# A metaformer kernel with gathers on GpSimd: readers of PSUM wait for a slot's last product

## The chip, the cores and the metric

The kernel runs on one core of one Trainium2 chip. The metric is the device time of one execution in microseconds (us); lower is better. The engines are called by their names in the profile where rows are quoted: PE is TensorE, DVE is VectorE, ACT is ScalarE, POOL is GpSimd, SP is SyncE; PEld is TensorE's loading of weights.

## What is computed

The reference is a network of two layers on four images of 128 channels and 128 x 128 pixels, in 32-bit floats. Layer 0 normalises, computes 18 offsets per pixel by a 3 x 3 convolution, reads each of nine taps at an offset position by bilinear interpolation, and multiplies the taps with a weight matrix (a deformable convolution). Its second half sends each token to the two best of eight experts. Layer 1 has a spectral convolution, which the kernel computes as products with a fixed matrix on flipped and plain channels, and a soft mixture of the eight best of 64 experts.

```python
def corner(iy, ix, w):
    valid = (iy >= 0) & (iy <= H - 1) & (ix >= 0) & (ix <= W - 1)
    iyc = jnp.clip(iy, 0, H - 1).astype(jnp.int32)
    ixc = jnp.clip(ix, 0, W - 1).astype(jnp.int32)
    g = jax.vmap(lambda img, yy, xx: img[:, yy, xx])(x, iyc, ixc)
    return g * (w * valid.astype(x.dtype))[:, None]
return corner(y0, x0, wy0 * wx0) + corner(y0, x1, wy0 * wx1) + corner(y1, x0, wy1 * wx0) + corner(y1, x1, wy1 * wx1)
...
return jnp.einsum('bckhw,ock->bohw', sampled, w_conv.reshape(O, C, K * K))
```

## The kernel before

**Slots.** An image is cut into 32 groups of four rows, and a row's nine taps into three chunks of three taps. One chunk is one slot: 12 slots to a group, 384 to an image, 1536 in the main loop (`while n < total + 3 or turns.jobs`, from L1588). The class `Chunk` (L729 to L786) holds what is done for one chunk, in the order of its life:

- `gather` (L737): three indirect DMAs, one per tap, issued by GpSimd. Each fetches for the 128 pixels of a row the four corners of 128 channels, out of a table in HBM, into the tile `g`. There are seven such tiles (`AHEAD`).
- `weighted` (L750): VectorE multiplies the corners by their weights, two taps or three. The weights are in the tile `spread`.
- `weighted_too` (L758): for chunks past the first of a row, ScalarE weights the third tap, with four activations.
- `summed` (L766): twelve transposes on TensorE, four per tap, add up the corners in a bank of PSUM, the tile `trg`.
- `moved` (L780): ScalarE copies `trg` to `sT` in SBUF; after the fourth row of a group a job is started that multiplies `sT` with the weights of the convolution, into the PSUM tile `sums`.

In slot n the loop does, in this order: `weighted` of chunk n+1, `moved` of chunk n-2, a step of each job that is due, the weights of a group, `weighted_too` of chunk n+1, `summed` of chunk n, the fillings of banks by jobs, and last the gather of chunk n+7, when the chunk is appended to the list.

**Jobs.** All other work (the experts, the normalisations, the offsets of the next image) is written as generators, which the class `Turns` (L114 to L156) resumes. A job yields `FILL` before it fills a bank and a number of slots before it reads one. In the main loop `turns.hop` is 2: a bank is read two slots after it was filled. Before and after the loop it is 1. A PSUM pool has six banks (`BANKS`); `fills` lets jobs fill no more than these in two slots. [...]

**Order.** `InOrder` (L91 to L103) wraps each engine and keeps its instructions in the order of the program, so every operation has the line L101 in the profile, and rows are told apart by their tiles. Semaphores are placed by the framework from reads and writes of tiles: a reader of a bank waits for the products that filled it, the next filling waits for the readers and the earlier products, and a gather waits for the transposes that read its tile `g` last.

```python
def issued(*args, **kwargs):
    return self.tc.keep_in_program_order(issue(*args, **kwargs))
```

Of the kernel before, what the change touches and what calls it, by code (L numbers as in the profile page):

```python
# [42 lines left out]
F32 = mybir.dt.float32  # L43
# [5 lines left out]
PSUM = bass.MemoryType.PSUM  # L49
# [41 lines left out]
class InOrder:  # L91


    def __init__(self, tc, engine):
        self.tc, self.engine = tc, engine

    def __getattr__(self, name):
        issue = getattr(self.engine, name)

        def issued(*args, **kwargs):  # L100
            return self.tc.keep_in_program_order(issue(*args, **kwargs))  # L101

        return issued  # L103


class Engines:
    def __init__(self, tc):
        nc = tc.nc
        self.tensor, self.vector = InOrder(tc, nc.tensor), InOrder(tc, nc.vector)
        self.scalar, self.gpsimd = InOrder(tc, nc.scalar), InOrder(tc, nc.gpsimd)  # L110
        self.sync = InOrder(tc, nc.sync)


# [73 lines left out]
def metaformer_kernel(  # L187
# [16 lines left out]
    nc = tc.nc  # L204
# [33 lines left out]
    with ExitStack() as main:  # L238
# [7 lines left out]
        p_x = main.enter_context(tc.tile_pool(name="p_x", bufs=BANKS, space=PSUM))  # L246
# [2 lines left out]

        def bank(shape, name):  # L250

            return p_x.tile(shape, F32, name=name, tag="bank")

        eng = Engines(tc)
        turns = Turns()
# [4 lines left out]
        class Image:  # L260


            def __init__(self, b):
                self.b = b
                self.table = tabs.tile([TW * TC, 2 * P], F32, name=f"table{b}", tag="table")
                self.grid = self.table.rearrange("(i j) e -> i j e", j=TC)
                self.index = pw.tile([P, P, TAPS], I32, name=f"index{b}", tag="index")
                self.weight = {}
                self.xc = {}
                self.z = {}  # L270
                self.tails = {}


                self.read = self.normed = self.continued = self.sent = 0
                self.offsets = self.placed = self.known = 0
                self.left = 0
                self.direct = P // RB
                self.rooms = {}

            def room(self, q):  # L280
                return pw.tile(
                    [P, CB, TAPS, 4],
                    F32,
                    name=f"weight{self.b}_{q}",
                    tag="weight",
                    bufs=3 * P // CB // 2,
                )
# [372 lines left out]
        def table_of(im, pitch):  # L660

            base = turns.slot
            im.left = P // RB + 1 + P // CB
            for t in range(P // RB + 1):
                while turns.slot < base + int(t * pitch):
                    yield 1
                turns.start(block(im, t))

        def later_offsets(im):
            for t in range(im.direct, P // RB):  # L670
                turns.start(again(im, t))
                yield SPACE
# [56 lines left out]
        class Chunk:  # L729
# [7 lines left out]
            def gather(self):  # L737
                self.g = pg.tile([P, 3, 4, P], F32, name="g", tag="g")
                for i in range(3):
                    k = self.k0 + i  # L740
                    eng.gpsimd.indirect_dma_start(
                        out=self.g[:, i].rearrange("p s c -> p (s c)"),
                        out_offset=None,
                        in_=self.row.group.im.table,
                        in_offset=bass.IndirectOffsetOnAxis(
                            ap=self.row.group.im.index[:, self.row.y, k : k + 1], axis=0
                        ),
                    )

            def weighted(self):  # L750
                n = 2 if self.shared else 3
                gf = self.g[:, 0:n].rearrange("p k s c -> p (k s) c")
                w = self.row.group.w[:, self.row.s, 4 * self.k0 : 4 * (self.k0 + n)]
                eng.vector.tensor_tensor(
                    gf, gf, w.unsqueeze(2).to_broadcast(list(gf.shape)), ALU.mult
                )
# [830 lines left out]
        n = -1  # L1587
        while n < total + 3 or turns.jobs:  # L1588
            turns.slot = start + n
            b, k = divmod(n, slots)  # L1590
            if n == 0:
                turns.start(later_offsets(first))
            lag = 0 if b else SPACE * (P // RB - AFTER + 2)
            if k == lag and b + 1 < NB:
                images[b + 1] = Image(b + 1)
                images[b + 1].border()
                pitch = (slots - AHEAD - BLOCK - lag) / (P // RB)
                turns.start(table_of(images[b + 1], pitch))
            if n + 1 < total:
                chunk[n + 1].weighted()  # L1600
            if 0 <= n - 2 < total:
                chunk[n - 2].moved()
            turns.steps()
            if n >= 0 and n + 3 < total and (n + 3) % 12 == 0:
                chunk[n + 3].row.group.weights((n + 3) // 12 % 2)
            if n + 1 < total and chunk[n + 1].shared:
                chunk[n + 1].weighted_too()
            if 0 <= n < total:
                chunk[n].summed()
                turns.fill()  # L1610
            turns.fills(0)
            if n == LATE * slots:

                phase_a.close()
                late = main.enter_context(tc.tile_pool(name="late", bufs=2, side="right"))
                b1T = late.tile([P, NJ, E1], F32, name="b1T", tag="b1T", bufs=1)
                b2T = late.tile([P, E1], F32, name="b2T", tag="b2T", bufs=1)
                turns.start(biases(), later=True)
                part = lambda: late.tile([P, 2, HID], F32, name="w", tag="w", bufs=4)

                rooms = [[part(), part()], [part(), part()], flat_pads]
                rooms.append([pw.tile([P, 2, HID], F32, name="w", tag="index")])
                for _ in range(2):
                    rooms[-1].append(
                        pw.tile([P, 1, HID], F32, name="w", tag="weight", bufs=3 * P // CB // 2)
                    )
                middle = Experts(range(LATE), Weights(lambda i: rooms[i % 4]), 4, 2)
                middle.part = part
                middle.streams = 2
                middle.weights.load(4)  # L1630
                middle.start()
            if 0 <= n - 2 < total:
                chunk[n - 2] = None
            if 0 <= n and len(chunk) < total:
                chunk.append(next(source))
            n += 1
            if n == total + 2:
                turns.hop = 1

                sampling.close()  # L1640
                own = main.enter_context(tc.tile_pool(name="own", bufs=OWN))

                flat = lambda w: w[:, 0:8, :].rearrange("p (n q) c -> p n (q c)", q=4)
                others = [
                    flat_pads,
                    [(late, f"{tile}{b}") for tile in ("tok", "share") for b in (1, 2)],
                    [flat(wconv_sb), flat(ew_sb)],
                ]

                def room(i):  # L1650
                    i %= OWN + 3 + len(LEFT)
                    if i < OWN:
                        return own.tile([P, EC, HID], F32, name="w", tag="w")
                    i -= OWN
                    if i == 1:
                        return [
                            pool.tile([P, 1, HID], F32, name="w", tag=tag, bufs=1)
                            for pool, tag in others[1]
                        ]
                    if i < 3:  # L1660
                        return others[i]
                    return [
                        pb.tile([P, n, HID], F32, name="w", tag=tag, bufs=bufs)
                        for tag, n, bufs in LEFT[i - 3]
                    ]

                ending = Ending(range(LATE, NB), Weights(room), OWN + 2, 1)
                ending.part = lambda: own.tile([P, 2, HID], F32, name="w", tag="w")
                ending.streams = OWN // 2
                ending.among = False  # L1670
                turns.start(ahead())
                ending.start()
# [39 lines left out]
```

## Time and profile before

| what | value |
|---|---|
| median of three runs | 7361.9 us (7357.83 to 7363.09) |
| the profiled execution, its own time | 7358.05 us |
| span in its profile, first to last instruction | 7356.1 us |
| mean granted clock of TensorE | 0.896 |
| busy: TensorE, VectorE, ScalarE, GpSimd | 82%, 65%, 50%, 60% |
| gathers by GpSimd | 4608, of 950 ns |
| copies of `trg` to `sT` by ScalarE | 1536, of 472 ns |
| transposes into `trg` | 18432 |

A group row of the profile has the line, the engine, the operation, the tiles written and read with their shapes, and the count; after the first bar the busy time and the mean duration in ns; after the second the time that the engine sat idle just before these instructions, and what ended most of it. "issue" there is time in which an engine waited for nothing that the profile shows, and "remote" a signal whose sender it doesn't name. A row of the timeline has the start, the duration, the engine, the operation and its tiles, and in brackets the idle time before it. In the 40 slices of the span the shares hardly change from the second slice to the last but one: TensorE is 80 to 90% busy in most, GpSimd 60%. 1536 slots fill nearly the whole span.

### The profile page before, as it was taken

The page shows a single profiled execution, that of the slowest core. Times are in us where ns is not written, and L with a number is a line of the kernel's source. Part 1 is how long each engine was busy: PE and PEld are TensorE (multiplying, and loading weights), DVE is VectorE, ACT ScalarE, POOL GpSimd, SP SyncE. Part 2 cuts the span into 40 slices and gives each one's busy share as a digit, 9 for nine tenths or more (in the row PEclk, how much of TensorE's full clock was granted, in tenths as well). Part 3 has the DMA queues.
Part 4 walks back from the last instruction along what each step waited for, and adds up shares of the span by engine and source line. Part 5 has one row for each costly group of instructions (what it writes and reads, how often), then busy time and mean ns, then how long its engine had stood idle before and what let it go on. Part 6 is the DMA issues. An engine that isn't in the chain of part 4 may idle for free. (4 is left out here: it accounts for less than half of the span.)

```text
span 7356.1 us, 103037 instructions
## 1 busy us (share of the span) xinstructions
PE 6006.3 (82%) x31271; PEld 3981.9 (54%) x31271; DVE 4789.5 (65%) x16100; ACT 3707.7 (50%) x9999; POOL 4432.3 (60%) x4691
## 2 busy tenths in 40 slices
PE   5788888887888888887888888888877788788885
PEld 3455555555555555555555555555555555555553
DVE  5466666676667666666667666667667665566663
ACT  4345555554555555554455555555444444444452
POOL 1666666666666666666666666666666665666641
PEclk7888999998898998998899999898898999899897
DMA  6666666666666666666666666666666677677777
GB/s 204 191 200 212 204 207 210 202 194 188 197 201 203 205 206 200 204 193 186 193 209 200 207 202 201 198 199 210 186 189 181 201 250 238 180 247 237 246 236 273
DMA packets 578917, 1524.69 MB, mean 207 GB/s; under 512 B 86424, under 2 KB 225408, under 8 KB 578368
## 3 DMA queue, kind: packets, MB, share of 16 engines
q0 software_dynamic: 369664, 1210.35, 55.0%
q1 hardware_dynamic: 206400, 299.36, 12.1%
q10 hardware_dynamic: 2304, 8.39, 0.3%
q8 instruction: 254, 4.16, 0.2%
q14 instruction: 295, 2.42, 0.1%
HBM read 1380.92 MB, written 136.85 MB: 206 GB/s over the span
## 5 line engine op out<-in xcount | busy, mean ns | idle before, releaser
L101 POOL DMA_INDIRECT g<-table,index x4608 | 4377.4, 950 | 2710.4 <-issue 1190.9
L101 PEld LDWEIGHTS trg<-ident,g 128*128 128x128 f32 x18432 | 2300.2, 150 | 1501.3 <-issue 1288.2
L101 PE MATMUL trg<-ident,g 128*128 128x128 f32 x18432 | 2575.2, 288 | 562.9 <-issue 465.9
L101 DVE SCALAR_TENSOR_TENSOR x<-pe,scaled,x 128x128 f32<-128x128 f32 x4048 | 1379.7, 341 | 1432.5 <-remote 644.6
L101 DVE TENSOR_TENSOR g<-g,spread 128x1024 f32<-128x1024 f32 (+1 forms) x1536 | 2129.1, 1387 | 202.4 <-DMA g<-table,index 90.0
L101 ACT COPY sT<-trg 128x384 f32<-128x384 f32 x1536 | 720.5, 472 | 2742.1 <-remote 1187.4
L101 PE MATMUL sums<-sT,wconv_sb 128*128 128x512 f32 x2304 | 1326.6, 658 | 53.1 <-issue 50.9
L101 ACT ACTIVATE g<-g,weight 128x128 f32<-128x128 f32 x4096 | 1306.3, 394 | 1.9 <-DMA g<-table,index 1.7
L101 PE MATMUL pe<-ew_sb,x1T 128*128 128x512 f32 x2048 | 1163.6, 649 | 147.0 <-issue 88.6
L101 PEld LDWEIGHTS sums<-sT,wconv_sb 128*128 128x128 f32 x2304 | 435.1, 208 | 518.9 <-issue 516.5
L101 PEld LDWEIGHTS pe<-ew_sb,x1T 128*128 128x128 f32 x2048 | 343.7, 205 | 261.1 <-issue 182.3
L101 ACT ACT_TABLE_LOAD x270 | 346.4, 1283 | 23.5 <-DVE nmax L101 9.8
L101 PE MATMUL sums<-xg,ident 128*128 128x512 f32 x256 | 163.8, 726 | 125.8 <-ACT x1T L101 96.8
L101 DVE TENSOR_TENSOR x<-ps,x 128x512 f32<-128x512 f32 x128 | 88.1, 688 | 264.5 <-remote 119.6
L101 PE MATMUL po<-pad,woff_sb 128*64 128x512 f32 x768 | 216.1, 645 | 17.8 <-issue 11.0
L101 DVE TENSOR_TENSOR x<-x,pe 128x512 f32<-128x512 f32 x128 | 87.0, 679 | 217.8 <-remote 130.4
L101 PE MATMUL pl<-rw_sb,x1T 128*128 128x8 f32 x1024 | 143.9, 256 | 98.2 <-issue 88.7
L101 ACT ACTIVATE tn<-x,d_nb,d_rs 128x128 f32<-128x128 f32 x512 | 211.2, 487 | 5.5 <-DVE x L101 2.6
L101 ACT ACTIVATE xn<-x,c_nb,c_rs 128x128 f32<-128x128 f32 x512 | 210.6, 485 | 4.7 <-issue 1.8
L101 PEld LDWEIGHTS pl<-rw_sb,x1T 128*128 128x128 f32 x1024 | 147.3, 213 | 98.5 <-issue 88.6
L101 ACT ACTIVATE ent<-raw,a_nb,a_rs 128x128 f32<-128x128 f32 x448 | 185.0, 485 | 7.6 <-remote 3.8
L101 PE MATMUL pe<-eb_sb,gT 32*128 32x512 f32 x256 | 169.4, 740 | 20.0 <-issue 14.6
(227 smaller groups left out, 5130.9 us busy)
## 6 DMA issues: line engine op xcount, KB each, us to landing
g<-table,index POOLq DMA_INDIRECT x4608
table<-ent SPq DMA_DIRECT2D x64, 1024.0 KB
xc<-in_x SPq DMA_DIRECT2D x64, 512.0 KB
w<-x_d SPq DMA_DIRECT2D x64, 512.0 KB
xg<-in_x SPq DMA_DIRECT2D x124, 256.0 KB
x_d<-x SPq DMA_DIRECT2D x124, 256.0 KB
out<-w SPq DMA_DIRECT2D x48, 512.0 KB
w<-in_weight SPq DMA_DIRECT2D x40, 512.0 KB
```

The lines of the kernel that those rows point to most:

```text
L101: return self.tc.keep_in_program_order(issue(*args, **kwargs))
```

## The change

The wrappers of the engines get state. `Fills`, on TensorE, keeps the last product issued, the last product of each of the last three slots (`ends`), and the products that went into each tile. `Readers`, on VectorE, ScalarE and GpSimd, looks at each instruction that reads a PSUM tile which TensorE filled:

- The first such reader of a slot on ScalarE, and the first on VectorE, gets a wait for `ends[-2]`, the last product of two slots ago. This holds in the main loop only (`turns.hop` over 1). Later readers in the slot are behind it in their engine's order.
- A reader that reads at least four fifths of a tile, or a tile with one product only, becomes its fence: the products of the tile are put in a group without dependencies among them, and the reader stands for it. The bank's next filling waits for that reader.
- The first of a chunk's three gathers gets a wait for `ends[-1]`, the last product of the slot that has just been issued.

The loop marks the first readers as `fresh` at the start of each slot and calls `eng.tensor.end()` after the fillings. No arithmetic, no transfer and no tile is changed.

```diff
+class Fills(InOrder):
+    def __init__(self, tc, engine):
+        super().__init__(tc, engine)
+        self.last, self.ends = None, []
+        self.sizes, self.of = {}, {}
...
+            made = issue(*args, **kwargs)
+            self.last = made.ins
+            self.of.setdefault(args[0].name, []).append(made.ins)
+            return made
...
+    def end(self):
+        self.ends = self.ends[-2:] + [self.last]
+
+class Readers(InOrder):
...
+    def behind(self, made, end):
+        self.tc.add_manual_dep(
+            made.ins,
+            end.name,
+            mybir.DependencyInfo(mybir.DependencyClass.Sync, mybir.DependencyReason.DATA),
+        )
+
+    def read(self, made, a):
+        if self.fresh:
+            self.behind(made, self.fills.ends[-2])
+            self.fresh = False
+        made_of, size = self.fills.of[a.name], self.fills.sizes.get(a.name)
+        if size and (len(made_of) == 1 or 5 * a.free_size() >= 4 * size):
+            for ins in made_of:
+                self.tc.add_to_no_dep_group(a.name, ins)
+            self.tc.declare_fence(made.ins, group=a.name)
+            del self.fills.sizes[a.name]
...
+            for a in list(args) + list(kwargs.values()):
+                if isinstance(a, bass.AP) and a.space == PSUM and a.name in self.fills.of:
+                    self.read(made, a)
+                    break
...
 class Engines:
     def __init__(self, tc):
         nc = tc.nc
-        self.tensor, self.vector = InOrder(tc, nc.tensor), InOrder(tc, nc.vector)
-        self.scalar, self.gpsimd = InOrder(tc, nc.scalar), InOrder(tc, nc.gpsimd)
+        self.tensor = Fills(tc, nc.tensor)
+        self.vector, self.scalar, self.gpsimd = (
+            Readers(tc, engine, self.tensor) for engine in (nc.vector, nc.scalar, nc.gpsimd)
+        )
...
-            return p_x.tile(shape, F32, name=name, tag="bank")
+            tile = p_x.tile(shape, F32, name=name, tag="bank")
+            eng.tensor.sizes[tile.name] = tile.free_size()
+            return tile
...
-                    eng.gpsimd.indirect_dma_start(
+                    made = eng.gpsimd.indirect_dma_start(
...
+                    if i == 0 and eng.tensor.ends:
+                        eng.gpsimd.behind(made, eng.tensor.ends[-1])
...
             turns.slot = start + n
+            for engine in (eng.vector, eng.scalar):
+                engine.fresh = turns.hop > 1 and len(eng.tensor.ends) > 1
...
             turns.fills(0)
+            eng.tensor.end()
```

More of the change, by code (lines that the diff above doesn't have):

```diff
@@ L103, in __getattr__, with issued, __init__ @@
         return issued
+class Fills(InOrder):
[3 more added lines that the diff above has]
+        self.sizes, self.of = {}, {}
+    def __getattr__(self, name):
+        issue = super().__getattr__(name)
+        def issued(*args, **kwargs):
+            made = issue(*args, **kwargs)
+            self.last = made.ins
+            self.of.setdefault(args[0].name, []).append(made.ins)
+            return made
+        return issued
+    def end(self):
+        self.ends = self.ends[-2:] + [self.last]
+class Readers(InOrder):
+    def __init__(self, tc, engine, fills):
+        super().__init__(tc, engine)
+        self.fills, self.fresh = fills, False
+    def behind(self, made, end):
[14 more added lines that the diff above has]
+            del self.fills.sizes[a.name]
+    def __getattr__(self, name):
+        issue = super().__getattr__(name)
+        def issued(*args, **kwargs):
+            made = issue(*args, **kwargs)
+            for a in list(args) + list(kwargs.values()):
+                if isinstance(a, bass.AP) and a.space == PSUM and a.name in self.fills.of:
+                    self.read(made, a)
+                    break
+            return made
+        return issued
 class Engines:
```

## The prediction

> **What bounds the kernel now.** I read the page's busy shares first, then the group rows, the waits, the timelines of GpSimd and ScalarE in one stretch of the main loop, and last a stretch of the start without gathers.
>
> ```profile
> PE 6006.3 (82%) x31271; PEld 3981.9 (54%) x31271; DVE 4789.5 (65%) x16100; ACT 3707.7 (50%) x9999; POOL 4432.3 (60%) x4691
> ...
> L101 POOL DMA_INDIRECT g<-table,index x4608 | 4377.4, 950 | 2710.4 <-issue 1190.9
> ...
> L101 ACT COPY sT<-trg 128x384 f32<-128x384 f32 x1536 | 720.5, 472 | 2742.1 <-remote 1187.4
> ```
>
> No engine is full. ScalarE is half idle, and of that idle time 2742 us lie before one group, the copy of `trg` out of PSUM.
>
> GpSimd's timeline (start, duration, what ended the idle time) shows how a slot is paced:
>
> ```profile
> 3009.06 0.95 POOL L101 DMA_INDIRECT g<-table,index  x1 [0.30 <-issue]
> 3012.09 0.95 POOL L101 DMA_INDIRECT g<-table,index  x1 [2.08 <-ACT gT L101]
> 3013.34 0.95 POOL L101 DMA_INDIRECT g<-table,index  x1 [0.30 <-issue]
> ...
> 3017.10 0.95 POOL L101 DMA_INDIRECT g<-table,index  x1 [0.30 <-issue]
> 3018.36 0.95 POOL L101 DMA_INDIRECT g<-table,index  x1 [0.30 <-issue]
> ```
>
> Gathers run in rows with 0.30 us between them: 1.2525 us each, 3.757 us for a slot's three. Then comes a pause. Over the trace 4608 x 1.2525 = 5771 us, and 626 pauses add 1214 us (1.94 us each, beyond the 0.30); together 6985, and about 371 us lie at the start and end: the span of 7356.1. 1536 slots over 626 pauses are 2.45 slots per run, so a slot takes 3.757 + 1.94/2.45 = 4.55 us; 4481 gathers in the 6800 us from 200 to 7000 give the same. GpSimd is the chain, and its pauses are what can be had.
>
> Why does it pause? Each chunk's gather waits for a product. TensorE and ScalarE in the same stretch:
>
> ```profile
> 3015.14 1.47 PE L101 MATMUL trg<-ident,g 128*128 128x128 f32 x12
> ...
> 3017.75 1.47 PE L101 MATMUL trg<-ident,g 128*128 128x128 f32 x12
> ```
>
> ```profile
> 3015.38 1.28 ACT L101 ACTIVATE g<-g,weight 128x128 f32<-128x128 f32 x4
> 3020.68 0.48 ACT L101 COPY sT<-trg 128x384 f32<-128x384 f32 x1 [4.02 <-PE trg L101]
> ```
>
> The `trg` that this copy reads is complete at 3016.61, yet the copy starts at 3020.68, 1.4 us after the run's last gather ended (3018.36 + 0.95 = 19.31). Where no gather runs the signal is immediate:
>
> ```profile
> 59.59 3.48 PE L101 MATMUL po<-pad,woff_sb 128*64 128x512 f32 x11
> ```
>
> ```profile
> 63.11 0.59 ACT L101 COPY os<-po 128x512 f32<-128x512 f32 x1 [1.24 <-PE po L101]
> ```
>
> That `po` ends at 63.07, the copy starts at 63.11. By the trace's semaphore records a signal of TensorE comes 14 ns after its row in the first 120 us and after 7160; from 200 to 7000 the median is 3.2 us, the 95th percentile 9. Within a run of gathers about half the signals of its first 2.5 us are late, 99% after 5 us; the rest arrive in a burst 1.4 to 2 us after its last gather. The waits give the bill:
>
> ```profile
> POOL g L101 <- issue: 1190.9, 3496, 5.0
> ACT sT L101 <- remote: 1187.4, 262, 15.6
> ...
> ACT sT L101 <- PE trg L101: 597.7, 204, 16.8
> ```
>
> So GpSimd runs until it needs a signal that its own run has held back; it pauses, the signals burst out, it goes on.
>
> **What the delay is made of.** Inside runs two signals close together come 1.45 us apart in all, three 2.16, four 2.90; a fit over all pairs gives 0.61 us per signal and 0.146 us per product. TensorE issues 6022 semaphore updates, 3.92 a slot, beside 21 products: 3.92 x 0.61 + 21 x 0.146 = 5.5 us of service per slot. A run makes a slot in 3.757, so the backlog grows by 1.74 us a slot, and a run of 2.45 slots ends with 1.74 x 2.45 = 4.3 us of it: the slack that I call L.
>
> **The change part by part.** *Removed:* waits of later readers in a slot (ScalarE waits for TensorE 2669 times, VectorE 1442, GpSimd 1532) and TensorE's 923 waits on itself for a bank. Those 923 are satisfied 1.7 us or more before they are needed: worth 0, and nothing is due if the cover goes, since TensorE is in order. The readers' waits matter through the signals that they oblige TensorE to send. After the change ScalarE, VectorE and GpSimd all wait for one product a slot, the last: 1 signal. SyncE's 311 waits stay (0.2). About 383 slots send four single updates, because third taps are weighted by ScalarE one by one; if they stay, 1.0. Together 2.2; the bounds are 1.2, and 2.8 if all 4313 updates that anyone awaits today stay. I take 2.2, since nothing in the diff touches those singles. Service is then 2.2 x 0.61 + 3.07 = 4.4 us, growth 0.65 us a slot.
>
> The Trainium skill prices this otherwise: "TensorE: Matmul & The Clock Gate", section "The cost: per-tile semaphore tail", has increments serialise at 26.3 ns each. By it, (3.92 - 2.2) x 1536 x 26.3 ns = 69 us are saved at most: 7290. The burst, at 42 ns per update, is near that rule; inside runs the trace has 610 ns. As 78% of the span (5771 of 7356) lies in runs, I take the trace.
>
> *Added, GpSimd:* the chunk's first gather waits for the slot's last product instead of `trg`. Behind it stand the two other gathers and all later ones; their data is used six slots later, so only the pause itself costs. The fills after `trg` take 1.7 us on average. Of 606 gathers that begin a run 351 would wait further, by 0.09 us at the median, 60 to 144 us in all. This shortens L by 0.1 to 1.7; I take 1.7, the whole slot end.
>
> *Added, ScalarE and VectorE:* the first reader, mostly `sT<-trg`, waits for the end of slot n-2 instead of its `trg`. Behind it on ScalarE stand the `spread` copies and the four activations for the next transposes, for which TensorE waits. With signals as late as now 480 of 1493 copies would start over 0.3 us later, 1396 us in sum (0.9 a slot); with signals at once 354 us (0.24). I take 0.45 a slot, as if it shortened L too. On VectorE it is 45 to 238 us, off the chain: with about 3.0 us of work a slot it has room down to there. No arithmetic, transfer, bank or buffer changes.
>
> So L = 4.3 - 1.7 - 0.45 = 2.1 us, runs last 2.1/0.65 = 3.25 slots, a slot takes 3.757 + 1.94/3.25 = 4.35: 0.195 x 1536 = 300 us less. The profiled execution took 7358.1 (2 us around its span), the median 7361.9; the forecast is 7060.
>
> A second rule speaks against the change: the same page, "Why this matters for your kernels", wants no idle gap over about 3 us on TensorE, or its clock halves. The trace has 244 half-clock spells, costing 816 us, 3.3 each. TensorE's longest waits reach 8 us already and each 1000 us has a granted clock of 0.89 to 0.91. If later copies make 40 more spells, 130 us come back: 7190. I take none, because shorter pauses remove gaps too.
>
> **How low it can go.** With 1.2 signals service is 3.8, about the pace of the gathers, and TensorE binds: from its rows between 200 and 7000 us, over 1494 slots, 4760 us of products at full clock, 816 of half clock and 416 of waits for ScalarE, 4.02 a slot: 6550.
>
> **Rivals.** *Slower:* the later waits cost and the fewer signals don't pay: lateness goes with rows and gathers, not with updates. For it: signals come in one burst after a run, however many. Against: their steady 0.72 us spacing inside runs. Then growth stays 1.74; L shortened by 0.3 gives 2.3 slots a run, +90 us, by 1.0 1.9 slots, +370. Nearest the direct 60 to 144 us plus some ScalarE: +150, 7510. It decides where growth falls by less than L does: with half of L lost, as I take it, growth must fall under 0.87, service under 4.6 us: 2.6 signals a slot; with a third lost, 3.0.
>
> *No effect:* the update that matters, the slot's last, comes in the same burst as `trg` now, and starts the same gathers: 7362, within 0.2% (about what a measurement of this kernel can tell from no change). For it: bursts deliver everything within 0.1 to 0.5 us. Against: the exact balance it needs between earlier and later.
>
> *It doesn't do what it says:* a fence could leave the old waits standing, and updates stay at 2.8 or more; that ends as the slower case.
>
> **How the numbers follow.** Faster through fewer signals 0.62 (2.7 to 6 slots a run: 6640 to 7250), no effect 0.08, slower 0.30 (7380 to 7730). Below 6750 I leave 0.07, above 7500 0.12: the range is 6750 to 7500.
>
> **What would show it.** Right: some 2 updates a slot, fewer than 500 pauses of GpSimd, idle time before `sT<-trg` well under 2742 us, a median delay of signals under 3 us. Wrong: pauses over 626 or over 1.94 us each; few updates and signals late as before would break the cost per signal; 2.8 or more updates would break the count.

## The result, and the profile after

The changed kernel takes 7455.5 us (median of 4 runs, 7450.35 to 7456.69), the kernel before 7362.5 on the same chip: a ratio of 1.0123, with an interval of 1.0106 to 1.0141. It is 93 us slower; the forecast was 300 us faster. The rows of the page that answer to those of before:

```profile
PE 6006.0 (81%) x31271; PEld 3992.5 (54%) x31271; DVE 4787.2 (64%) x16100; ACT 3683.2 (49%) x9999; POOL 4432.9 (59%) x4691
...
L101 POOL DMA_INDIRECT g<-table,index x4608 | 4378.0, 950 | 2802.1 <-issue 1166.6
...
L101 ACT COPY sT<-trg 128x384 f32<-128x384 f32 x1536 | 723.3, 473 | 3461.4 <-remote 2165.2
```

The work is the same to a few us on every engine but ScalarE, which is busy 24 us less, and a gather still takes 950 ns. What grew is idle time: 92 us before the gathers (2710 to 2802) and 719 us before the copy of `trg`. The first number is about the loss of 93 us. From the first gather to the last the trace has 7081.2 us instead of 6989.3, and by the prediction's own accounting, a pause being any gap over 0.5 us between gathers:

| kernel | pauses | mean gap, us | pauses beyond 0.30, us in all | span, us |
|---|---|---|---|---|
| before | 628 | 2.227 | 1210 | 7356.1 |
| after | 619 | 2.400 | 1300 | 7454.6 |

So there are about as many pauses, and each is 0.17 us longer: +90 us of the span's +98.5.

What a pause ends with has changed. GpSimd and ScalarE in the same stretch of the changed kernel:

```profile
3008.97 0.94 POOL L101 DMA_INDIRECT g<-table,index  x1 [0.30 <-issue]
3012.63 0.95 POOL L101 DMA_INDIRECT g<-table,index  x1 [2.72 <-DVE d_nb L101]
...
3026.42 0.95 POOL L101 DMA_INDIRECT g<-table,index  x1 [0.30 <-issue]
3030.65 0.95 POOL L101 DMA_INDIRECT g<-table,index  x1 [3.28 <-ACT sT L101]
```

```profile
3011.88 0.48 ACT L101 COPY sT<-trg 128x384 f32<-128x384 f32 x1 [5.13 <-remote]
...
3029.90 0.48 ACT L101 COPY sT<-trg 128x384 f32<-128x384 f32 x1 [5.08 <-remote]
```

The copies end at 3012.36 and 3030.38, and the gathers start 0.27 us after each. The first gather's row names VectorE, which is only what the releaser was inferred to be. Matched with the waits in the built program, 592 of 596 gathers that end a pause between 200 and 7000 us wait last for a copy `sT<-trg`, and nearly all start 0.27 us after it. In the kernel before, 606 of 613 wait last for TensorE's signal. The waits of the changed kernel, and below them a row of the kernel before:

```profile
ACT sT L101 <- remote: 2165.2, 382, 15.3
...
POOL g L101 <- issue: 1166.6, 3663, 4.2
...
POOL g L101 <- ACT sT L101: 693.6, 281, 5.2
```

```profile
POOL g L101 <- ACT sT L101: 367.7, 157, 6.9
```

The shift is there, but this view can't prove it: it names the copy for 367.7 us in the kernel before as well, where no gather waits for it.

The waits in the two built programs say why. GpSimd waits for TensorE 1532 times before and twice after. In 1529 chunks the first gather now waits for ScalarE's copy of the chunk whose tile `g` it refills. The copy is the fence of `trg`, and it stands for the twelve transposes not only towards the bank's next filling, but towards everyone who waits for them, the gather included. The wait for the slot's last product, which the diff adds to the gather, is covered by this later one, and the built program no longer has it: that is why two waits for TensorE are left, and not 1532.

### The profile page after: what moved, and what is told of

Same layout as the page of the kernel before. It is cut to its first block, busy times and chain, and to the rows that moved or that the text cites. A ratio compares the mean times of both kernels' runs of the same rounds, so it can differ in the third digit from the quotient of the medians.

```text
span 7454.6 us, 102045 instructions
## 1 busy us (share of the span) xinstructions
PE 6006.0 (81%) x31271; PEld 3992.5 (54%) x31271; DVE 4787.2 (64%) x16100; ACT 3683.2 (49%) x9999; POOL 4432.9 (59%) x4691
```

## The experiments

Two groups of four ran, each on one chip. The kernel before took 7286.0 us on the first chip and 7276.2 on the second; every ratio is against it on the same chip. The expectations of the first group are on the scale of 7362, so they are to be read as distances from that. In the diffs, lines with + and - are against the kernel named.

**The fence of `trg` alone** (against the changed kernel):

```diff
-        if size and (len(made_of) == 1 or 5 * a.free_size() >= 4 * size):
+        if size and a.name.startswith("trg"):
...
-                    if i == 0 and eng.tensor.ends:
+                    if False:
...
-                engine.fresh = turns.hop > 1 and len(eng.tensor.ends) > 1
+                engine.fresh = False
```

> The kernel of before with one part of the change: the copy of trg out of PSUM is the fence of trg's bank; no wait for first readers, no wait of gathers added. In the built program the first gather of a chunk then no longer waits for TensorE's transposes but for ScalarE's copy sT<-trg of the same chunk, which stands two slots later in the program. TensorE's updates stay at 6018 (3.92 a slot). Theory G (this moved wait is the loss): slower than before by 1% or more, 7440 to 7560, with longer pauses of GpSimd put down to ScalarE. Theory L (the loss comes from the first readers' later waits): within 0.3% of before, 7340 to 7385.

It took 7398.1 us, a ratio of 1.0150 (1.0133 to 1.0166). This one part is the whole loss; its interval overlaps that of the whole change. Pauses: 592 of 2.417 us, 1253 us beyond the 0.30; in the third run, on the same chip and without a fence, 1150. Of the gathers that end a pause 572 of 577 wait last for the copy.

**Everything but that fence** (against the changed kernel):

```diff
-        if size and (len(made_of) == 1 or 5 * a.free_size() >= 4 * size):
+        if size and not a.name.startswith("trg") and (len(made_of) == 1 or 5 * a.free_size() >= 4 * size):
```

> The change with every part but trg's fence: gathers wait for the last product of the slot, a signal of TensorE; updates 3955 (2.57 a slot instead of 3.92). Theory G: the loss is gone, at or below before, 7150 to 7362, and if a signal costs 0.61 us in a run of gathers as the prediction had it, below 7250. Theory L: still slower than before, 7400 to 7480.

7306.8 us, 1.0027 (1.0018 to 1.0037). The loss is gone but for 21 us (0.27%; theory G had expected none), which the next two runs account for (12 and 9 us, if they add up), and there is no gain, although TensorE sends 2.57 updates a slot instead of 3.92. With the forecast's cost of an update the run would have been over 110 us faster than before; that cost is refuted.

**The first readers' wait alone** (against the changed kernel; no tile gets a fence, and no gather the added wait):

```diff
-        if size and (len(made_of) == 1 or 5 * a.free_size() >= 4 * size):
+        if False:
...
-                    if i == 0 and eng.tensor.ends:
+                    if False:
```

> The kernel of before with only the wait of the first PSUM reader of a slot on ScalarE and VectorE for the last product of two slots ago; no fences, no wait of gathers added. Updates 5784, nearly as before, so the fewer signals are not there and the later wait is alone. Theory L: 7420 to 7480. Theory G: within 0.5% of before, 7330 to 7400.

7297.8 us, 1.0018 (1.0009 to 1.0028). The later wait costs 12 us, not 60 to 120 as the theory that lays the loss on it needs.

**The gathers' added wait alone** (against the changed kernel; no fence, no first readers):

```diff
-        if size and (len(made_of) == 1 or 5 * a.free_size() >= 4 * size):
+        if False:
...
-                engine.fresh = turns.hop > 1 and len(eng.tensor.ends) > 1
+                engine.fresh = False
```

> The kernel of before with only the gathers' wait for the last product of the slot instead of the transposes of trg; updates 6022, the same as before. The prediction's price for this wait alone is 60 to 144 us: 7420 to 7510. Theory G says that this wait is not even there in the changed kernel and expects 7380 to 7450 here. If signals arrive in bursts anyway, 7350 to 7380.

7295.4 us, 1.0013 (1.0003 to 1.0022). Here the wait is real, and it costs 9 us: below every range that was set down except the one for bursts. At the start of a run the gather comes some 2 us after its own `trg`'s signal on average, instead of some 0.7; yet the pauses are 606 of 2.194 us, against 629 of 2.129 in the run of the first readers, on the same chip and with the gathers' waits of before: hardly longer, and fewer.

**Plain transfers for gathers** (against the kernel before; it leaves out the offsets, taps are read at fixed places):

```diff
-                    eng.gpsimd.indirect_dma_start(
+                    eng.sync.dma_start(
                         out=self.g[:, i].rearrange("p s c -> p (s c)"),
...
+                        in_=self.row.group.im.table[self.row.y * TC : self.row.y * TC + 2 * P].rearrange(
+                            "(p q) e -> p (q e)", q=2
+                        ),
```

> The kernel of before with each gather replaced by a plain transfer of the same 256 KB on SyncE's queue, out of a fixed stretch of the table. It leaves out the offsets: the taps are not read where the reference reads them. The waits for a free tile are the same, SyncE has them. If gathers on GpSimd hold TensorE's signals back (the prediction's premise), the signals come 14 ns after their products and the time falls to TensorE's own sum, 6400 to 6700. If TensorE's signals are late by themselves in this loop, the time stays within 2% of before, 7150 to 7430.

5381.2 us, 0.7397 (0.7385 to 0.7409). The first rows of its page, and the copy's group:

```profile
PE 5209.2 (97%) x31271; PEld 3635.1 (68%) x31271; DVE 4752.4 (88%) x16100; ACT 3728.8 (69%) x9999; POOL 54.9 (1%) x83
...
PEclk8999999999999999999999999999999999999987
...
L101 ACT COPY sT<-trg 128x384 f32<-128x384 f32 x1536 | 722.6, 472 | 1027.0 <-PE trg L101 1012.5
```

The row of the granted clock in the kernel before:

```profile
PEclk7888999998898998998899999898898999899897
```

TensorE is busy 97% of the span and is the bound; its signals come 14 ns after their rows at the median and 15 ns at the 95th percentile, with 5847 updates and the same number of rows. So the premise holds: the signals are late because of the gathers. The run can't tell which side of a gather does it, its work on GpSimd or the indirect transfers themselves. The gain is far over what was set down, and not all of it is the signals': the gathers' own time on GpSimd is gone too, and 4608 of them in one row, at 1.2525 us each, would alone take 5771 us, more than this whole run. The half clock is nearly gone as well: 14 spells, 163 us in all, where the kernel before has 244 and 1538 us (a mean granted clock of 0.985 for 0.896). In this comparison the half clock went when TensorE's stalls went.

**A fence on `g`** (against the kernel before): the last transpose stands for VectorE's and ScalarE's weighting, so the gather waits for TensorE alone. In `weighted` and `weighted_too` the instructions are put into `self.writers`; then in `summed`:

```diff
-                        eng.tensor.matmul(
+                        made = eng.tensor.matmul(
...
+                for one in self.writers:
+                    tc.add_to_no_dep_group(self.g.name, one.ins)
+                tc.declare_fence(made.ins, group=self.g.name)
```

> The kernel of before with a fence of another kind: the last transpose of a chunk stands for all that touched its tile g, so the gather that fills the tile next waits for TensorE alone and no longer for VectorE's and ScalarE's weighting as well (those waits were met long before). In the trace of before 65% of the gathers that begin a run start 0.26 us after TensorE's signal and 35% 0.73 us after it, those where the wait for TensorE is followed by another wait instruction. If the step from signal to gather is paid at every pause (theory G in general), about 210 pauses get 0.47 us shorter: 60 to 100 us less, 7185 to 7235. If pauses end at another time anyway, 7270 to 7300.

7214.2 us, 0.9917 (0.9901 to 0.9934): faster than both kernels. In its timeline:

```profile
3002.99 0.95 POOL L101 DMA_INDIRECT g<-table,index  x1 [0.30 <-issue]
3005.62 0.94 POOL L101 DMA_INDIRECT g<-table,index  x1 [1.68 <-PE trg L101]
...
3011.99 0.95 POOL L101 DMA_INDIRECT g<-table,index  x1 [0.30 <-issue]
3014.42 0.94 POOL L101 DMA_INDIRECT g<-table,index  x1 [1.48 <-PE trg L101]
```

The idle time before a gather that ends a pause is 1.68 and 1.48 us here, 2.72 and 3.28 in the changed kernel's stretch. At least 80% of these gathers start 0.26 us after TensorE's signal. In the kernel before somewhat over half carry that wait in their own instruction, and most of these start 0.26 us after the signal too; for the other 270 the wait is in a wait instruction ahead, and nearly all take 0.73 (more than the 35% that the expectation had). 270 times 0.47 us would be 127 us, 62 came: the time was inside the forecast, but each pause gave about half of what was expected, from more pauses. Pauses: 702 of 1.836 us, 1078 us beyond the 0.30.

**Two copies, the control** (against the kernel before):

```diff
                 eng.scalar.copy(group.sT[:, :, s, :], self.tr)
+                eng.scalar.copy(group.sT[:, :, s, :], self.tr)
```

> Control for the next: the kernel of before, with the copy of trg out of PSUM made twice (0.47 us more of ScalarE a slot, same result). ScalarE is half idle and no gather waits for it: all theories expect within 0.7% of before, 7260 to 7340.

7290.0 us, 1.0015 (1.0006 to 1.0025). More work on ScalarE is nearly free, as long as no gather waits for it. Pauses: 642 of 2.097 us, 1154 us beyond the 0.30.

**Two copies with the fence** (against the control): as in the first experiment, and the second copy is the fence.

```diff
+    def again(self, name):
+        self.seen = getattr(self, "seen", set()) ^ {name}
+        return name not in self.seen
...
+        if size and a.name.startswith("trg") and self.again(a.name):
```

> The same with two copies, and the second copy is the fence of trg: gathers wait for ScalarE's second copy. Theory G, in its form that each pause is longer by the time from TensorE's signal to the end of the copy: twice the copy, so about twice the loss of one, 2.3 to 3.5% over the control, 7450 to 7580. If only the place of the copy two slots later in ScalarE's order counts and not its length: 1.3 to 1.8% over the control.

7579.7 us, 1.0418 of before (1.0400 to 1.0435), 290 us or 4.0% over the control (the quotient of the two medians), above the 2.3 to 3.5% that were set down. Pauses: 573 of 2.820 us, 1444 us beyond the 0.30. That is 290 us more than the control: the pauses account for the whole difference. GpSimd's rows in the waits of this kernel don't show it, since the inferred releaser is often another (for the control the view puts 479.8 us down to the copy):

```profile
POOL g L101 <- issue: 1122.1, 3601, 3.8
...
POOL g L101 <- ACT sT L101: 443.5, 195, 5.6
...
POOL g L101 <- DVE x L101: 335.9, 175, 5.6
```

One copy in the chain costs 1.5%, two 4.0%; taking a second wait out of it gives 0.8%. All three move the step from TensorE's signal to the next gather. At the start of a run it is 0.26 us for about half the gathers and 0.73 for over 40% in before and control; with the fence on `g` 0.26 for over 80%; at the median 0.77 with one copy and 1.28 with two. The means are longer, 1.4 and 2.1 us, for 0.7 in before and control: mostly ScalarE copies at once when the signal comes, but with one copy it starts 2.9 us or more after the signal in one case of ten. So the copy's place in ScalarE's order is paid beside its length. Only part of the step shows in the time: for two copies the median step grew by about 1.0 us and the mean by 1.4, the pause by 0.72 (against the control), and there are fewer pauses. Why that is so, and why two copies cost more than twice one, the runs leave open. A kernel with the fence on `g` and the first readers' waits together wasn't tried.

## Why the prediction was wrong, point by point

- **The bound: right.** GpSimd's rows of gathers and their pauses set the time; in every kernel that kept its gathers on GpSimd, the gaps moved with the time (1210 to 1300 us for before and after, 1154 to 1444 for the last two). That the signals are late because of the gathers, which the trace only suggested, is shown by the plain transfers.
- **The step that failed: "Added, GpSimd: the chunk's first gather waits for the slot's last product instead of `trg`."** It waits for ScalarE's copy of `trg`. I took the fence for something between a bank's reader and its next filling, and put its worth at 0, because TensorE's waits on itself never end last. That part is so. But the fence also took the place of the transposes in the gather's wait for its tile `g`, and put a copy of 0.47 us and ScalarE's own order between the signal and GpSimd, at nearly every pause (592 of 596). The fence of `trg` alone gives 1.0150, all the rest 1.0027.
- **The term that was mis-sized: 0.61 us per update.** The count was right, 2.2 forecast and 2.30 built (3528 updates), but it bought nothing: 2.57 a slot give 1.0027, 3.77 and 3.92 give 1.0018 and 1.0013. The fit that split the time into updates and rows couldn't tell them apart: repeated on the traces of the first four experiments it gives between about 0.3 and 0.9 us per update, depending on the kernel and on how signals are matched with rows. The time from the end of `trg` to the next signal is even longer on average in the changed kernel, by 0.6 to 0.9 us: with fewer signals, the next one belongs to a later product. Two of the prediction's own signs of being wrong came, pauses over 1.94 us and few updates without a gain. What sets the pace of the late signals instead stays open.
- **The added waits: right in sign, far too dear.** The gathers' wait was put at 60 to 144 us and costs 9, that of the first readers 12.
- **L, the slack, and the 3.25 slots per run.** Runs became no longer: 1536 slots over 619 pauses are 2.48, before 2.45. The model had only the run's length vary, with the pause fixed at 1.94 us beyond the 0.30. It is the pause that moved: 2.10 in the changed kernel, 1.54 with the fence on `g`, 2.52 with two copies and the fence (in these two with runs of 2.19 and 2.68 slots).
- **The rivals.** The slower rival's first number, +90 us, is what came, but by another mechanism, so the agreement is luck. It had the first readers' and gathers' later waits as the cause, and each alone costs a tenth of it. "It doesn't do what it says" had the fence in view, as one that leaves old waits standing; it replaced one that should have stood.
- **The floor of 6550 us** took half clock and waits for ScalarE as fixed. Its 816 us of half clock are too many: the spells last 1538 us, so at half speed they cost at most 769, and nearly all of them were gone in the run without gathers. The 5381 us without gathers on GpSimd are no floor for a kernel that has them: 5771 us of gathers and the 371 us at start and end are 6142.
- **The two rules** of the Trainium skill's page "TensorE: Matmul & The Clock Gate". The 26.3 ns per increment of "The cost: per-tile semaphore tail" gave at most 69 us and was nearer to the nothing that came than my 610 ns. That clock and gaps go together, as "Why this matters for your kernels" has it, no run here contradicts; the mean granted clock is 0.882 with two copies and the fence, 0.896 before, 0.909 with the fence on `g`, 0.985 without gathers on GpSimd.

## What to carry to other kernels

Where one engine works in bursts and pauses until a signal comes, what counts is the chain from that signal to its next instruction: an instruction put into it lengthens the pauses, however idle its engine is (here by roughly half of what it added to the step). Before a fence or a group of accesses is costed, list every reader of the instructions that it stands for, those through other tiles too, and look in the built program at whom each of them waits for. A cost per signal that is fitted where signals and rows come together should be tested by a run that changes only one of them, before a forecast rests on it.

## What the runs showed of the hardware

- While GpSimd issues gathers, TensorE's signals are late: about 3 us at the median, 14 ns with plain transfers on SyncE. With the plain transfers the half-clock spells are nearly gone too (1538 us before, 163 without gathers).
- Fewer semaphore updates by TensorE, 2.57 a slot instead of 3.92, brought no time beside the gathers (1.0027).
- A gather whose wait for the late signal is in the wait instruction ahead of it starts 0.73 us after the signal; one that carries the wait itself mostly starts after 0.26, and one that waits for ScalarE's copy 0.27 us after the copy's end.
